# Zero products during the first loads, keys first, later rows' normalization behind the scores, and one bare step more at three places of the chains

## The chip, the cores and the metric

The kernel runs on one core of one Trainium2 chip. The core has a matrix engine (TensorE, called PE in the profile), a vector engine (VectorE, DVE), an activation engine (ScalarE, ACT), a general engine (GpSimd, POOL) and an engine that mainly starts transfers (SyncE, SP). Each works off its own queue in order and waits for the others by semaphores. Products land in PSUM, a small memory of banks from which DVE or ACT has to fetch them before a bank can be used again. The metric is the device time of one execution in microseconds (us).

## The reference

Two layers of a perceiver. x has 16 batches of 64 rows of 256 numbers, the context 16 batches of 1024 rows of 256. There are 16 heads of 16 numbers each.

```
x = x + cross_attention_0(layernorm(x), ctx, mask)      # softmax(q k / sqrt(16)) v, then Wout
x = x + column_attention(layernorm(x))                  # softmax with 1 + sum, rotary, causal
x = x + moe(layernorm(x))                               # 8 experts, 2 of them for each row, by capacity
x = x + cross_attention_1(layernorm(x), ctx, bias, mask)
x = x + row_attention(layernorm(x))                     # within each batch of 64 rows, rotary
x = x + fp4_feed_forward(layernorm(x))                  # silu(gate) * up, operands rounded to fp4 by blocks of 16
```

All is float32; the fp4 step is a rounding of float32 numbers to a grid of eight magnitudes, with a scale for each block of 16.

## The kernel before, in words

The 1024 rows of x are eight tiles of 128 rows, a tile being two batches (a pair). The layers follow each other: layer 0's cross attention (about 38 to 520 us of the profiled execution), column attention (to about 650), the experts (to about 870), then layer 1's cross attention, into which the row attention and the feed forward of finished pairs are woven (to about 1425), and a tail of what the last pairs still need.

**The order of work.** PE's order in the cross attention is the order in which the code issues it (the engine is under `manual_schedule`). The other engines' queues are ordered by a scheduler. Where the code says `issue_after`, an instruction's place is put behind a named other one.

**The main loop** of `cross_attention` (L331 to L761, the loop at L719) runs over 64 slots, four to a batch b: two halves of the heads (dt) by two halves of the keys (hf). One turn of the loop issues
- `scores` of the slot two ahead: four products (L567) into four banks, and for each a DVE instruction (L578) that adds the mask and finds the extremum (tile mn). Each second slot has also the four exponentials on ACT (L589);
- four k-steps of its own slot: `transpose_keys` (four transposes L597 into one bank, fetched by DVE at L226 or by ACT at L228), each followed by `advance()`. Between them come steps of projections for later batches: `project` (L394 for keys, L409 for values), or in layer 0 for most batches `project_seven` (L458, L462), a product by seven products instead of eight that needs sums of context made by POOL (`sum_context`, L448);
- `attend` of the slot before (L611, 32 products into the accumulating bank).

Seven banks go round among all users, and one is kept for `attend`.

**The chains.** `advance()` takes one step of every running chain. A chain is a Python generator, and each of its `yield`s leaves PE to one k-step of the loop before the chain's next piece; `bare(n)` (L250) is n yields with nothing between. The chains are
- `queries(n)`: `layernorm_rows` (L255: bn_stats at L258, bn_aggr at L260, three Newton steps for the inverse root, the rows xnq at L275 on DVE or L281 on POOL), two transposes (L290, fetched by ACT at L292), the query product (L527) and qm on ACT (L537), which the scores of the next pair need. It starts at the third of a pair's eight slots for the pair after;
- `outputs(b)` (L619) after a batch's last `attend`: ot, the transposes L633, osb (L636), and for the second batch of a pair some bare yields, the transposes L648, oT on DVE (L652), two yields, and `project_rows` (L322), the output product that goes into x;
- in layer 1 then `row_attention(n)` (qkv at L1371, L1391 and L1414, scores L1426, exponential ra on ACT at L1444, transposes L1450, L1465, L322 again) and `feed_forward(n)` (normalization, fp4 rounding on DVE, transposes L290, the hidden products L1517 in two halves, Silu on ACT (L1520), the product with up on DVE (L1521), fp4 rounding (L1036 to L1052), transposes L1527, the down product L1542).

exp and Silu are functions of different tables on ACT, and each change between them issues an ACT_TABLE_LOAD.

**Layer 0's end.** When the slots are finished, the remaining chain goes on with prepared layer-1 projections between its steps (`idle`, which calls `make_ahead`, L782 and L795); keys and values of most batches of layer 1 are prepared in this way or during the column attention. In layer 1 the remaining batches' projections (L394, L409) stand in the main loop: the later four pairs have them, the first three have not.

**The start.** The first loads are issued by ACT's and SP's queues: the key half of the weights w_L_xattn_Wkv, the first rows of x, column constants, the query weights, the value half, and the first context. Then, in PE's order: the first projection step (L394) of batch 0, a step of `queries(0)` (transposes L290), the second projection step, the rest of `queries(0)`, the scores of slots 0 and 1, and the other six steps (two for keys, four for values).

Of the kernel before, what the change touches and what calls it, by code (L numbers as in the profile page):

```python
# [9 lines left out]
F32 = mybir.dt.float32  # L10
# [110 lines left out]
def kernel(ctx: ExitStack, tc: tile.TileContext, a: dict, out: bass.AP):  # L121
# [17 lines left out]
    def bank():  # L139
        return psum["w"].tile([P, 512], F32, name="psw")  # L140
# [46 lines left out]


    w0kv = wpool.tile([P, KC, 2 * D], F32, name="w_L0_xattn_Wkv")
    w0kv_in = a["L0_xattn_Wkv"].rearrange("(c p) n -> p c n", p=P)  # L190
    nc.scalar.dma_start(w0kv[:, :, :D], w0kv_in[:, :, :D])
    nc.scalar.dma_start(x[0], xf[:P, :])
# [57 lines left out]
    def bare(n):  # L250

        for _ in range(n):
            yield

    def layernorm_rows(pool, n, name="xnr", vector=False):  # L255

        st = small.tile([P, 6], F32, name="bnst")
        nc.vector.bn_stats(st, x[n])  # L258
        mv = small.tile([P, 2], F32, name="mvr")
        nc.vector.bn_aggr(mv, st)  # L260
        va = small.tile([P, 1], F32, name="var")
        nc.vector.tensor_scalar(va, mv[:, 1:2], EPS, None, ALU.add)

        half = small.tile([P, 1], I32, name="half")
        nc.vector.tensor_scalar(half, va.bitcast(I32), 1, None, ALU.logical_shift_right)
        r = small.tile([P, 1], F32, name="rsd")
        nc.vector.tensor_scalar(r.bitcast(I32), half, -1.0, 1597463007.0, ALU.mult, ALU.add)
        t = small.tile([P, 1], F32, name="nwt")
        xn = pool.tile([P, D], F32, name=name)
        if vector:  # L270
            nc.vector.tensor_scalar(va, va, -0.5, None, ALU.mult)
            for _ in range(3):
                nc.vector.tensor_scalar(t, r, va, r, ALU.mult, ALU.mult)
                nc.vector.scalar_tensor_tensor(r, t, 1.5, r, ALU.add, ALU.mult)
            made[name] = nc.vector.tensor_scalar(xn, x[n], mv[:, 0:1], r, ALU.subtract, ALU.mult)  # L275
            return xn
        for _ in range(3):
            nc.gpsimd.tensor_scalar(t, r, va, r, ALU.mult, ALU.mult)
            nc.gpsimd.tensor_scalar(t, t, -0.5, 1.5, ALU.mult, ALU.add)
            nc.gpsimd.tensor_tensor(r, r, t, ALU.mult)  # L280
        made[name] = nc.gpsimd.tensor_scalar(xn, x[n], mv[:, 0:1], r, ALU.subtract, ALU.mult)  # L281
        yield
        yield
        yield
        return xn
# [45 lines left out]
    def cross_attention(layer, wq, wkv, wo, bq, bk, bv, bo, mask, keep, bias, after, ready, arrive, idle):  # L331
        side = "right" if layer else "left"
        with ExitStack() as st:
# [180 lines left out]
            def queries(n):  # L514


                arrive(n, two, 1)
                xn = yield from layernorm_rows(single, n, "xnq", layer == 1 or n == 0)
                if layer:
                    nc.gpsimd.tensor_tensor(x[n], x[n], rowbias(bo), ALU.add)  # L520
                    yield from bare(6 if n else 0)
                xT = transposed_rows(single, xn, "xTq")
                yield from bare(3 if layer else 2)
                pm = bank()
                for dt in range(KC):
                    for c in range(KC):
                        nc.tensor.matmul(  # L527
                            pm[:, dt * P : (dt + 1) * P],
                            wq[:, c, dt * P : (dt + 1) * P],
                            xT[:, c, :],  # L530
                            start=(c == 0),
                            stop=(c == KC - 1),
                        )
                qm[n] = two.tile([P, KC, 2, 2, SQ], F32, name="qm")
                for dt in range(KC):
                    for j in range(2):
                        nc.scalar.activation(  # L537
                            qm[n][:, dt, :, j, :],
                            pm[:, dt * P : (dt + 1) * P].rearrange("p (b q) -> p b q", q=SQ),
                            AF.Identity,  # L540
                            scale=const("parq")[:, j : j + 1],
                            bias=bqm[:, j, dt : dt + 1],
                        )
# [10 lines left out]
            def scores(b, dt, hf):  # L554
# [19 lines left out]
                for g in range(NG):  # L574
                    pr = dt * NG + g
                    e = es[b, dt, g]

                    nc.vector.tensor_tensor_reduce(  # L578
                        out=e[:, cols],
                        in0=sc[g],  # L580
                        in1=negb[b][:, cols],
# [37 lines left out]
            def outputs(b):  # L619
# [21 lines left out]
                    )  # L641
                if half == 0:
                    return
                yield from bare(3 if layer else 2)
                pt = bank()
                rows = osb[n].rearrange("p r j d -> p (r j d)")
                for c in range(KC):
# [2 lines left out]
                for c in range(KC):  # L650
# [1 line left out]
                    nc.vector.tensor_scalar(  # L652
                        oT[:, c, :], pt[:, c * P : (c + 1) * P], colbias(bv, c), None, ALU.add
                    )
                yield
                yield
                project_rows(n, oT, wo, None if layer else rowbias(bo))


# [39 lines left out]
            with tc.manual_schedule(engines={mybir.EngineType.PE}):  # L699
                arrive(0, two, 0)  # L700
                chains.append(queries(0))
                if 0 not in ready:
                    project(0, 0)
                    advance()
                    project(0, 1)
                while chains:
                    advance()
                if not layer:
# [5 lines left out]
                scores(*slots[0])  # L714
                scores(*slots[1])
                if 0 not in ready:
                    for step in range(2, NP):
                        project(0, step)
                for i in range(len(slots) + 1):  # L719

# [628 lines left out]
    def last_layers(one):  # L1349
# [148 lines left out]
        def feed_forward(n, two):  # L1498
# [4 lines left out]
            yield from fp4(fp4_tiles(one, "h", NI), xn, xn, P, D)  # L1503
            yield from bare(2)
            xT = transposed_rows(two, xn)
            yield
            yield
            h = one.tile([P, NI], F32, name="h")
            hT = one.tile([P, NCH, P], F32, name="hT")

# [174 lines left out]
```

## Time and profile before

| what | value |
|---|---|
| median of 3 runs | 1512.32 us (1509.17 to 1513.48) |
| profiled execution, its own time | 1521.49 us |
| its span, first to last instruction | 1519.5 us |
| PE busy in the span | 92% |
| DVE busy | 63% |
| ACT busy | 49% |
| POOL busy | 22% |
| mean granted PE clock | 0.955 |
| first matmul | 7.18 us |
| main loop of layer 0 begins | 38.10 us |
| table loads on ACT | 22 |

How to read it: times in the profile are microseconds from the first instruction of the profiled execution, which took 9.17 us more than the median of the runs. Differences inside the profile are taken from it alone, and only the sum is set against the median. A line of a timeline gives the start, the duration of a group of equal instructions, the engine, the line of the code, the operation, what it writes and reads, shapes, and the count; in brackets stand the idle time ahead of it and what ended that. The granted clock is 1.00 at full rate. A matmul of float32 is recorded as several passes, so that one projection step shows as four matmuls.

### The profile page before, as it was taken

What the parts mean: (1) busy time and instruction counts of PE and PEld (TensorE: products, weight loads), DVE (VectorE), ACT (ScalarE), POOL (GpSimd) and SP (SyncE); (2) the same over time, 40 slices, a digit from 0 to 9 for tenths busy, and PEclk for the clock granted to TensorE, in tenths of its full rate; (3) what the DMA queues carried; (4) which work ended last, traced back from release to release, by engine and by line L of the source; (5) the groups of instructions that cost most, each with busy time, mean ns of one, the idle gap of its engine ahead of it and who ended that gap; (6) DMA issues with size and microseconds to landing.
All of it is one profiled execution on the core that took longest, in us unless ns stands there. A gap on an engine that the chain in (4) does not pass through costs nothing.

```text
span 1519.5 us, 33552 instructions
## 1 busy us (share of the span) xinstructions
PE 1391.2 (92%) x13796; PEld 994.4 (65%) x13796; DVE 961.1 (63%) x2573; ACT 744.7 (49%) x1373; POOL 338.5 (22%) x368
## 2 busy tenths in 40 slices
PE   6999999999999898899999888979799999999854
PEld 3677667776777655668888555756566767676642
DVE  3677676767677524355730167587878687877654
ACT  2565566566665632123221376546565556565420
POOL 4343444344332021012300121111221111110000
PEclk9999999999999999999999899788999999999967
DMA  6111111121001122276882533222211111100000
GB/s 232 60 35 34 60 33 33 36 60 32 33 30 36 56 92 71 93 236 212 260 303 92 180 108 99 75 80 89 78 46 49 50 53 49 43 5 1 5 1 7
DMA packets 53557, 119.53 MB, mean 79 GB/s; under 512 B 4909, under 2 KB 25005, under 8 KB 51101
## 3 DMA queue, kind: packets, MB, share of 16 engines
q1 hardware_dynamic: 50732, 112.21, 22.4%
q0 software_dynamic: 1568, 4.26, 1.0%
q8 instruction: 108, 1.77, 0.5%
q10 hardware_dynamic: 1104, 0.93, 0.2%
q14 instruction: 45, 0.36, 0.1%
HBM read 94.32 MB, written 23.07 MB: 77 GB/s over the span
## 4 chain that ended last, share of the span: by engine, by line
PE 70%; DVE 16%; issue 5%; ACT 5%; DMA 3%; POOL 1%; ACTq 0%; DVEq 0%; POOLq 0%; SPq 0%
PE psw L597 10%; PE psw L567 8%; PE pso L611 7%; PE psw L458 6%; DVE e L578 5%; PE psw L462 5%; PE psw L795 4%; PE psw L1226 4%; PE psw L1246 4%; ACT e L589 4%; PE psw L394 3%; PE psw L782 3%; PE psw L1517 3%; PE psw L409 2%; PE psw L1542 2%
## 5 line engine op out<-in xcount | busy, mean ns | idle before, releaser
L589 ACT ACTIVATE e<-e,mn 128x1024 f32<-128x1024 f32 x256 | 291.1, 1139 | 119.1 <-DVE mn L578 119.1
L597 PEld LDWEIGHTS psw<-consts,e 128*128 128x128 f32 x2048 | 240.3, 143 | 102.9 <-issue 58.5
L597 PE MATMUL psw<-consts,e 128*128 128x128 f32 x2048 | 288.2, 279 | 10.5 <-ACT e L589 5.8
L228 ACT COPY eT<-psw 128x512 f32<-128x512 f32 x384 | 209.5, 588 | 176.3 <-PE psw L597 176.0
L578 DVE CUSTOM_DVE_ANT_0 e<-psw,negb,mn 128x512 f32<-128x512 f32 x256 | 178.5, 747 | 144.7 <-PE psw L567 144.7
L578 DVE CUSTOM_DVE_ANT_0 e<-psw,negb 128x512 f32<-128x512 f32 x256 | 163.8, 685 | 67.9 <-PE psw L567 67.4
L567 PE MATMUL psw<-kT,qm 32*128 32x512 f32 x1024 | 171.9, 659 | 11.1 <-ACT qm L537 6.6
L611 PE MATMUL pso<-eT,v 128*32 128x128 f32 x4096 | 140.9, 280 | 0.0
L611 PEld LDWEIGHTS pso<-eT,v 128*32 128x32 f32 x4096 | 106.2, 111 | 22.3 <-issue 21.9
L567 PEld LDWEIGHTS psw<-kT,qm 32*128 32x128 f32 x1024 | 53.5, 190 | 48.8 <-issue 20.1
L226 DVE COPY eT<-psw 128x512 f32<-128x512 f32 x128 | 82.8, 680 | 3.4 <-PE psw L597 3.4
L795 PE MATMUL psw<-w_L_xattn_Wkv_w,actx 128*128 128x256 f32 x288 | 74.6, 413 | 1.5 <-ACT astage L789 0.8
L359 POOL TENSOR_SCALAR negb<-m 128x1024 f32<-128x1024 uint8 x16 | 16.7, 1045 | 253.1 <-DVE mn L578 202.8
L782 PE MATMUL psw<-actx,w_L_xattn_Wkv_w 128*128 128x512 f32 x144 | 67.4, 608 | 1.3 <-DVE x L768 1.3
L795 PEld LDWEIGHTS psw<-w_L_xattn_Wkv_w,actx 128*128 128x128 f32 x288 | 58.7, 208 | 14.8 <-issue 4.2
L789 ACT ACTIVATE astage<-psw,colb 128x512 f32<-128x512 f32 x36 | 24.6, 686 | 80.8 <-PE psw L782 46.8
L462 PEld LDWEIGHTS psw<-wgT,actx 128*128 128x128 f32 x448 | 53.3, 192 | 10.6 <-issue 5.3
L462 PE MATMUL psw<-wgT,actx 128*128 128x128 f32 x448 | 58.3, 278 | 0.0
L1226 PE MATMUL psw<-xeT,w 128*128 128x256 f32 x256 | 56.6, 379 | 0.8 <-issue 0.8
L1246 PE MATMUL psw<-w,hT 128*128 128x256 f32 x256 | 56.6, 379 | 0.0
L458 PE MATMUL psw<-actx,wgT 128*128 128x512 f32 x112 | 56.4, 605 | 0.0
L1233 ACT ACTIVATE hT<-psw 128x512 f32<-128x512 f32 x32 | 19.0, 597 | 75.4 <-PE psw L1226 75.4
(282 smaller groups left out, 2281.2 us busy)
## 6 DMA issues: line engine op xcount, KB each, us to landing
ctxT<-in_ctxT_dram SPq DMA_DIRECT2D x23, 1024.0 KB, 4.8
w<-in_L_ffn_w_dram SPq DMA_DIRECT2D x16, 1024.0 KB, 8.3
actx<-in_ctxT_dram SPq DMA_DIRECT2D x9, 1024.0 KB, 5.6
kd<-astage SPq DMA_DIRECT2D x36, 256.0 KB, 4.4
vd<-astage SPq DMA_DIRECT2D x36, 256.0 KB, 2.3
kT<-kd SPq DMA_DIRECT2D x9, 1024.0 KB, 7.0
v<-vd SPq DMA_DIRECT2D x9, 1024.0 KB, 4.7
ab<-in_fside_BxS_dram SPq DMA_DIRECT2D x32, 256.0 KB, 3.3
```

What stands on the lines that cost most here:

```text
L228: nc.scalar.copy(dst, src)
L458: nc.tensor.matmul(pm, a_, x_, start=True, stop=True)
L462: nc.tensor.matmul(pm[:, cols], x_[:, cols], a_, start=True, stop=True)
L567: nc.tensor.matmul(sc[g], qm[b // 2][r : r + 32, dt, b % 2, :, :].rearrange("p j q -> p (j q)"), kT[b][r : r + 32, dt, cols], start=True, ...
L578: nc.vector.tensor_tensor_reduce(out=e[:, cols], in0=sc[g], in1=negb[b][:, cols], scale=1.0, scalar=3e38 if hf == 0 else mn[b][:, 0, pr : ...
L589: nc.scalar.activation(e, e, AF.Exp, scale=-1.0, bias=mn[b][:, 1, pr : pr + 1], accum_out=sums[b][:, pr : pr + 1])
L597: nc.tensor.transpose(pt[:, g * P : (g + 1) * P], es[b, dt, g][:, k * P : (k + 1) * P], ident)
L611: nc.tensor.matmul(po[b][32 * g : 32 * g + 32, dt, :], v[b][:, k, pr * 32 : (pr + 1) * 32], e[:, g, :], start=(k == 0), stop=(k == NK - 1),)
L782: nc.tensor.matmul(pm, w1kv[:, c, dt * P : (dt + 1) * P], actx[b][:, c, cols], start=(c == 0), stop=(c == KC - 1),)
L795: nc.tensor.matmul(pm[:, j * D : (j + 1) * D], actx[b][:, c, (k + j) * P : (k + j + 1) * P], w1kv[:, c, D : 2 * D], start=(c == 0), stop=( ...
L1226: nc.tensor.matmul(ph[:, j * CAP : (j + 1) * CAP], w1[:, c, (f + j) * P : (f + j + 1) * P], xeT[:, c, :], start=(c == 0), stop=(c == KC - 1),)
L1246: nc.tensor.matmul(py[:, j * D : (j + 1) * D], hT[:, f, j * P : (j + 1) * P], w2[:, f, :], start=(f == 0), stop=(f == FF // P - 1),)
```

## The change

There are four edits.

1. At the start of layer 0 three products of a tile of zeros are issued on PE into fresh banks ahead of the first projection. The tile is set by a DVE memset, which is the first instruction of DVE's queue. Nothing reads these banks before they are used again.
2. The first two projection steps come ahead of the transposes of `queries(0)`, and the third comes right after them; five instead of six steps follow the first scores.
3. In layer 0 the bn_stats of rows 1 to 7 (`layernorm_rows`) are put behind the last L578 that had been issued when `queries(n)` was started (`made["sc"]`).
4. Three numbers of bare steps grow by one: in layer 0 ahead of the transposes L648, in layer 1 ahead of `project_rows` of the cross attention (L322), and in `feed_forward` ahead of the hidden products (L1517).

```diff
     w0kv = wpool.tile([P, KC, 2 * D], F32, name="w_L0_xattn_Wkv")
+    zeros = wpool.tile([P, 1, P], F32, name="zeros")
+    nc.vector.memset(zeros, 0.0)
...
-    def layernorm_rows(pool, n, name="xnr", vector=False):
+    def layernorm_rows(pool, n, name="xnr", vector=False, behind=None):
         st = small.tile([P, 6], F32, name="bnst")
-        nc.vector.bn_stats(st, x[n])
+        with tc.issue_after(behind.ins) if behind else nullcontext():
+            nc.vector.bn_stats(st, x[n])
...
                 arrive(n, two, 1)
-                xn = yield from layernorm_rows(single, n, "xnq", layer == 1 or n == 0)
+                xn = yield from layernorm_rows(
+                    single, n, "xnq", layer == 1 or n == 0, made["sc"] if n and not layer else None
+                )
...
-                    nc.vector.tensor_tensor_reduce(
+                    made["sc"] = nc.vector.tensor_tensor_reduce(
...
                 if half == 0:
                     return
-                yield from bare(3 if layer else 2)
+                yield from bare(3)
                 pt = bank()
...
-                yield
-                yield
+                yield from bare(3 if layer else 2)
                 project_rows(n, oT, wo, None if layer else rowbias(bo))
...
                 if 0 not in ready:
+                    for _ in range(3):
+                        nc.tensor.matmul(
+                            bank().rearrange("p (k n) -> p k n", n=P),
+                            zeros[:, 0, :],
+                            zeros.to_broadcast([P, 4, P]),
+                            start=True,
+                            stop=True,
+                        )
                     project(0, 0)
+                    project(0, 1)
                     advance()
-                    project(0, 1)
+                    project(0, 2)
...
                 if 0 not in ready:
-                    for step in range(2, NP):
+                    for step in range(3, NP):
                         project(0, step)
...
             xT = transposed_rows(two, xn)
-            yield
-            yield
+            yield from bare(3)
             h = one.tile([P, NI], F32, name="h")
```

## The prediction

> **What bounds the kernel now.** I read the page first, then busy time by stretches, then the waits of TensorE (PE) in the two attention stages, then the first 40 us and the last 65 us instruction by instruction, and last ScalarE's (ACT's) table loads.
>
> ```profile
> PE 1391.2 (92%) x13796; PEld 994.4 (65%) x13796; DVE 961.1 (63%) x2573; ACT 744.7 (49%) x1373; POOL 338.5 (22%) x368
> ```
>
> ```profile
> core 0: us, PE busy (x) PEld busy (x) DVE busy (x) ACT busy (x) POOL busy (x), PEclk, DMA share, GB/s
> 24.00:30.00 6.00, 6.00 (x8) 2.19 (x7) 3.65 (x12) 4.33 (x7) 2.65 (x12) 0.50 0.84 310
> 120.00:400.00 280.00, 274.69 (x2792) 200.30 (x2795) 201.70 (x492) 173.52 (x327) 115.38 (x111) 1.00 0.13 40
> 1430.00:1520.00 90.00, 51.05 (x444) 34.60 (x443) 44.13 (x135) 15.56 (x28) 2.90 (x4) 0.74 0.02 5
> ```
>
> PE is the bound: 92% busy overall, 98% in the first cross attention (120 to 400). There a microsecond of PE waiting is a microsecond. From 1430 it is half idle, and chains of dependent steps set the time.
>
> ```profile
> 7.18 3.78 PE L394 MATMUL psw<-ctxT,w_L_xattn_Wkv 128*128 128x512 f32 x4 [7.18 <-DMA w_L_xattn_Wkv<-in_L_xattn_Wkv_dram]
> ...
> 12.85 0.69 PE L290 MATMUL psw<-consts,xnq 128*128 128x128 f32 x2 [1.90 <-DVE xnq L275]
> 13.34 3.38 PE L394 MATMUL psw<-ctxT,w_L_xattn_Wkv 128*128 128x512 f32 x4
> 16.55 1.05 PE L527 MATMUL psw<-xTq,w_L_xattn_Wq 128*128 128x128 f32 x8
> 18.50 1.99 PE L567 MATMUL psw<-kT,qm 32*128 32x512 f32 x14 [0.90 <-ACT qm L537]
> 23.19 2.07 PE L567 MATMUL psw<-kT,qm 32*128 32x512 f32 x2 [2.69 <-DVE mn L578]
> 25.19 6.07 PE L394 MATMUL psw<-ctxT,w_L_xattn_Wkv 128*128 128x512 f32 x8
> 31.10 7.07 PE L409 MATMUL psw<-w_L_xattn_Wkv,ctxT 128*128 128x256 f32 x32
> 38.10 1.14 PE L567 MATMUL psw<-kT,qm 32*128 32x512 f32 x8
> ```
>
> The start: PE begins when the first weights land (7.18), multiplies slowly, waits 1.90 for normalized rows and 2.69 for the first maximum of VectorE (DVE), and reaches the main loop at 38.10. Four matmuls of a projection (one step) take 3.78 or 3.38 here, 1.98 once the granted clock is full; the row 24 to 30 shows 0.50 granted.
>
> ```profile
> PE psw L648 <- DVE osb L636: 9.3, 7, 1.3
> ...
> PE psw L322 <- DVE oT L652: 12.0, 7, 2.2
> PE psw L1517 <- ACT xTr L292: 11.1, 6, 4.1
> PE psw L567 <- ACT qm L537: 4.8, 4, 2.2
> ```
>
> PE's waits (total, times, longest), the first of layer 0 (40 to 540), the others of layer 1 (900 to 1425). The first three waiters are moved.
>
> ```profile
> L1520 ACT ACT_TABLE_LOAD x8 | 10.3, 1283 | 0.1
> L589 ACT ACT_TABLE_LOAD x6 | 7.7, 1283 | 0.1
> ```
>
> ```profile
> 1474.36 0.53 ACT L228 COPY hT<-psw 128x256 f32<-128x256 f32 x2 [5.45 <-PE psw L1527]
> 1474.91 1.28 ACT L1444 ACT_TABLE_LOAD   x1
> 1476.20 1.06 ACT L1444 ACTIVATE ra<-ra 128x1024 f32<-128x1024 f32 x1
> 1477.31 1.97 PE L1450 MATMUL psw<-consts,ra 128*128 128x128 f32 x8 [2.99 <-ACT ra L1444]
> ```
>
> A table load (1283 ns) accompanies each change between exp and Silu. In the tail the last pair's exp (1476.20) holds PE's L1450.
>
> **The change, part by part.**
>
> *Start.* Three products of zeros are 6 matmul records at about 0.85 (L394's slow rate), an estimate of 5.1 us, before 7.17 when PE only waits; they need one DVE memset, so they cost nothing unless the memset comes after 2. Two steps now stand ahead of the transposes L290, so the 1.90 wait is filled. The later rows' bn_stats come behind the first scores' L578, so DVE (BATCH_NORM rows until 22.44) is free for the first scores at once. If the clock is full when the weights land: steps 0 and 1 from 7.18 to 11.2 (2 x 1.98), L290 at 12.85 (xnq ends at 12.80), step 2 to 15.3, L527 to 16.4, qm (1.5 in ACT, 17.64 to 19.14 before) with its 0.9 wait, scores from 17.3, paced at the end by the bank that the first L578 frees (18.0 + 0.7), done at 19.3. One key step (1.98) and four value steps (7.07 / 4) remain, and the main loop begins at 28.2 instead of 38.10: 9.9 won. If the clock stays slow until 14, the two steps end at 14.7, L290 and step 2 follow, and the gain is 8; if slow until 25, only the two waits and some 0.5 of overlap go: 5. Bounds 5 and 10.5; I take 9.9, since the zeros fill the stretch in which PE was idle.
>
> The Trainium skill, "TensorE: Matmul & The Clock Gate", Part 1, says that idling is the throttled default and that one busy free-running window of about 3.4 us releases it. The trace agrees in part: the clock is half from 23.17 to 29.99 in pieces of 3.41 us, after the idle 2.69. By that rule 5.1 us of zeros need not hold a whole window, and the start would go between the first two cases above.
>
> *Layer 0, L648 (seven pairs).* The transposes move past 16 L611 products, 4 L567, 8 L462 and one group of 4 transposes L597, over 3 us, and osb was 1.3 late: 9.3 removed. L322 follows two steps later as before, but oT (L652) now queues among L578: PE wants it at about 120.3 of the pair around 120, oT comes at 120.5 to 120.8, so 0.3 each. The normalization of rows 1 to 7 now runs in the rows' own slot: xnq (1.22 on GpSimd, POOL) ends, by POOL's order with L490 (1.27) ahead of it, at about 127.9, while PE wants L290 at 127.9 to 128.4: 0.2 each, and qm behind it 0.1. Net 9.3 - 7 x 0.6 = 5.1. Bounds: +9.3 if neither waits; -6 if both wait 1.1 more (a POOL operation's 1.22). Before, the rows lay ready a slot group ahead. At the end of layer 0 L322 has one prepared step more ahead of it and one less behind: bounds 0 and -1.7 (one step), I take -0.3, as 2 follow still. SP's and POOL's queues keep their DMAs but for small swaps.
>
> *Layer 1, L322 and L1517.* By pair L322 waits 1.02, 2.23, 2.23 and then 1.61 four times; L1517 waits 4.09 twice and 0.73 four times. In the four later pairs a slot also carries projection steps of nearly 2 us (L394, L409), so one yield more covers either wait: 4 x (1.61 + 0.73) = 9.4. In the early pairs L322 passes only one group of 4 transposes (0.44): 3 x 0.44 = 1.3; L1517 passes two such groups, L611 (1.08) and L567 (1.07), some 2.9 of its 4.09: 5.8. But there DVE and ACT are nearly as full and the next wait is theirs (L567 for qm already: 4.8), so I count half, 3.5, between 0 and 7.1.
>
> *Table loads.* In the changed order the second half's Silu falls behind the exps of the next slot: the program has 34 loads for 22, 12 more of 1.283 = 15.4 us of ACT, all in layer 1. ACT has slack there (49% overall), and qm (L537) behind a load is wanted some 3 us later in the projecting pairs; two early pairs lose 1.5 each: -3. Bounds 0 and -15.4.
>
> *Tail.* PE's order puts row 7's L1371, L1450 and L1465 ahead of row 6's L1517, L1542: L1450 comes 0.6 earlier, L1465 3.2, against chain steps of row 6 that come later. Bounds -1 and +5; I take +1.5, as row 6's down products (3.74) must still be done.
>
> **The sum.** 9.9 + 5.1 - 0.3 + 9.4 + 3.5 - 3 + 1.5 = 26.1. The profiled execution took 1521.49 (span 1519.5 and 2 around it), so 1495.4; it lies 9.17 above the median of 1512.32, whence 1486.2.
>
> **Rivals.**
> (A) Layer 1's gain is handed back: L1517 and L322 stop waiting, but PE next waits for banks that ACT and DVE free. DVE's waits for L567 there (a row of 66.6 us) speak against it, DVE is fed by PE; the early pairs speak for it. Without 9.4 + 3.5, less the loads' -3 now counted inside: 1486.2 + 9.9 = 1496.
> (B) All table loads on the path: 15.4 - 3 = 12.4 more than summed, 1498.6. For: four exps in a row ahead of a load leave Silu's two banks held, and PE has seven. Against: the exps there already end well ahead of PE in the projecting pairs.
> (E) A switch costs ACT twice its load, and all of it is on the path: 12 x 2 x 1.283 = 30.8, less 3, and 1514: within the measurement's bound. Against: between copy and exp in the rows above (1474.89 to 1476.20) lies nothing but the load.
> The Trainium skill, "ScalarE: Activation LUTs", "What ACT_TABLE_LOAD costs", speaks for (E): it gives about 1283 ns for the load and 1380 ns of drain, 2.66 us a switch, so 32 us for 12 (an estimate). The rows agree on the 1283 and show no drain.
> (C) Slower. Rows' normalization behind the scores makes xnq late at L290 for rows 2 to 7. PE's order is fixed, so all waits behind it. POOL decides: if sum_context's L448 products (5.1 us, 126.40 to 131.53) go ahead of xnq, six rows lose 5.1 each, 30.6, and 1517; with two L490 (2.55) more, 1532. It turns slower from 4.4 us a row on (26.1 / 6). For: the slack now used up was a slot group. Against: by POOL's order L448 stands behind xnq.
> (D) The zeros do not release the clock, so the start wins 5: 1491.
>
> **How the numbers follow.** Chances: forecast 0.47, A 0.17, B 0.09, C 0.10, D 0.15, E 0.02. The forecast's own range, from the terms' bounds taken in part, is 1478 to 1493. Leaving out half of C and the extremes of the others gives 1477 to 1508. A measurement here tells 0.3% (4.5 us) from no change: faster is under 1507.8, slower over 1516.9. A, D and the forecast are faster (0.79), B by half (0.04); the rest of B, E and a little of C fall within, C's rest (0.09) over it: 0.83 faster, 0.08 within, 0.09 slower.
>
> **What would show it.** L394 at 7.18 taking about 2 us for 4, the first L578 near 18 and the main loop near 28; L648 gone from layer 0's waits, no row of L290 waiting for xnq over 0.5 there; L322 and L1517 shrunk to the early pairs; 34 table loads, and L567's wait for qm grown by 3 at most; the last L1465 some 3 us nearer to row 7's scores. Wrong it would be by a row of L290 on POOL's xnq of tens of microseconds, or by L567 or L597 waiting for exps in layer 1.

## The result and the profile after

| | before | changed |
|---|---|---|
| median of 4 runs | 1512.9 us (1509.17 to 1521.0) | 1495.5 us (1492.21 to 1497.05) |
| profiled execution's span | 1519.5 us | 1490.3 us |
| table loads on ACT | 22 | 34 |

The changed kernel takes 0.9875 of the time, with a 95% interval of 0.9831 to 0.9919: faster by 1.2%. The forecast was 1486.2, in a range of 1477 to 1508. So the sign and the range held, and the gain is two thirds of the 26.1 us that were forecast. The two profiles are 29.2 us apart, against 17.4 of the medians; the section on the prediction comes back to this.

Lines of the changed kernel are shifted: L567 is now L574, L578 is L585, L597 is L604, L648 is L655, L322 is L326, L394 is L398, L1517 is L1531, L1527 is L1541 and L1542 is L1556; L290 is L294, L611 is L618, L1450 is L1465 and L1465 is L1480. In the runs below a line can lie a few places off these.

The busy shares of the page, of the changed kernel:

```profile
PE 1387.3 (93%) x13802; PEld 993.2 (67%) x13802; DVE 940.0 (63%) x2574; ACT 763.3 (51%) x1385; POOL 339.7 (23%) x368
```

The timeline of PE at the start, of the changed kernel (start, duration, count, and in brackets the idle time ahead):

```profile
1.05 4.41 PE L710 MATMUL psw<-zeros 128*128 128x512 f32 x6 [1.05 <-DVE zeros L192]
7.13 3.70 PE L398 MATMUL psw<-ctxT,w_L_xattn_Wkv 128*128 128x512 f32 x8 [1.68 <-DMA w_L_xattn_Wkv<-in_L_xattn_Wkv_dram]
12.84 0.44 PE L294 MATMUL psw<-consts,xnq 128*128 128x128 f32 x2 [2.01 <-DVE xnq L279]
13.12 1.88 PE L398 MATMUL psw<-ctxT,w_L_xattn_Wkv 128*128 128x512 f32 x4
...
16.79 3.15 PE L574 MATMUL psw<-kT,qm 32*128 32x512 f32 x16 [0.90 <-ACT qm L544]
...
28.69 1.14 PE L574 MATMUL psw<-kT,qm 32*128 32x512 f32 x8
```

The main loop begins at 28.69 instead of 38.10. Eight matmuls of L398 take 3.70, where four took 3.78.

PE's waits of the changed kernel (total, times, longest), from 40 to 535 and then from 880 to 1400:

```profile
PE psw L604 <- DVE mn L585: 2.6, 1, 2.6
PE psw L604 <- ACT e L596: 2.1, 3, 0.8
```

```profile
PE psw L326 <- DVE oT L659: 6.5, 7, 1.7
PE psw L1556 <- ACT hT L231: 5.3, 5, 2.0
PE psw L294 <- DVE xnr L279: 4.1, 3, 2.5
PE psw L604 <- DVE mn L585: 2.8, 2, 1.4
PE psw L1429 <- ACT h L1534: 2.7, 2, 1.3
```

The seven waits of L648 (9.3) and the waits of L1517 (11.1) are gone, and L322's fell from 12.0 to 6.5; in the later pairs 0.6 of each is left. In place of them stand one wait of 2.6 of L604 in layer 0, and in layer 1 waits for hT (5.3) and for Silu (L1534, 2.7), both from ACT.

**Where the time went.** I took the same product in both traces (the first of each eighth of the `attend` products, the first of each stage) and compared when it starts:

| stretch | difference, us |
|---|---|
| to the first slot's `attend` | -9.4 |
| layer 0, first pair to sixth | -7.4 (-1.73, then -1.11 to -1.14 each) |
| layer 0, seventh and last pair, and its end | +4.2 (+2.9 in the seventh, in which a wait of 2.56 stands) |
| column attention to the start of layer 1's `attend` | -5.9 |
| layer 1, pair 0; 1; 2 and 3 | 0.0; -6.8; +4.65 |
| layer 1, pairs 4 to 6; 7 | -2.3; -2.9 |
| tail | -3.4 |

The -5.9 lie in stages that the change doesn't touch. Some 3.6 of them go with the granted clock: before the experts' products the same work took 37.0 us at 0.82 in the profile before, 33.4 us at 0.90 in the one after. Another 2.2 lie in the column attention, 45.0 and 42.8 us at 0.92 both times, and stay unexplained. Single profiles differ by about this much: l322_alone and ff_step_alone (below), which leave everything up to layer 1 as it was, take 3.0 and 3.6 us less than the kernel before from layer 0's last `attend` to layer 1's first.

### The profile page after: what moved, and what is told of

Its sections match the earlier page's. It is cut to its first block, busy times and chain, and to the rows that moved or that the text cites. A ratio compares the mean times of both kernels' runs of the same rounds, so it can differ in the third digit from the quotient of the medians.

```text
span 1490.3 us, 33558 instructions
## 1 busy us (share of the span) xinstructions
PE 1387.3 (93%) x13802; PEld 993.2 (67%) x13802; DVE 940.0 (63%) x2574; ACT 763.3 (51%) x1385; POOL 339.7 (23%) x368
## 4 chain that ended last, share of the span: by engine, by line
PE 42%; DVE 10%; ACT 6%; issue 4%; DMA 2%; POOL 1%; ACTq 0%; DVEq 0%; POOLq 0%; SPq 0%
ACT e L596 4%; PE psw L604 4%; PE psw L1241 4%; PE psw L1261 4%; PE psw L810 4%; PE psw L574 4%; PE pso L618 3%; DVE e L585 3%; PE psw L398 2%; PE psw L413 2%; PE psw L797 2%; PE psw L1531 2%; DMA kd<-astage 2%; PE psw L1556 1%; PE psw L326 1%
## 5 line engine op out<-in xcount | busy, mean ns | idle before, releaser
L604 PEld LDWEIGHTS psw<-consts,e 128*128 128x128 f32 x2048 | 238.5, 142 | 104.5 <-issue 52.9
L604 PE MATMUL psw<-consts,e 128*128 128x128 f32 x2048 | 286.9, 278 | 13.1 <-DVE mn L585 6.6
L585 DVE CUSTOM_DVE_ANT_0 e<-psw,negb,mn 128x512 f32<-128x512 f32 x256 | 178.3, 746 | 129.6 <-PE psw L574 129.3
L585 DVE CUSTOM_DVE_ANT_0 e<-psw,negb 128x512 f32<-128x512 f32 x256 | 163.2, 686 | 67.6 <-PE psw L574 67.1
L574 PE MATMUL psw<-kT,qm 32*128 32x512 f32 x1024 | 175.6, 666 | 5.5 <-ACT qm L544 4.4
L618 PE MATMUL pso<-eT,v 128*32 128x128 f32 x4096 | 142.6, 282 | 0.0
L618 PEld LDWEIGHTS pso<-eT,v 128*32 128x32 f32 x4096 | 107.3, 112 | 23.5 <-issue 20.9
L574 PEld LDWEIGHTS psw<-kT,qm 32*128 32x128 f32 x1024 | 56.2, 191 | 44.0 <-issue 19.0
L466 PEld LDWEIGHTS psw<-wgT,actx 128*128 128x128 f32 x448 | 53.3, 192 | 10.6 <-ACT eT L231 10.6
L1248 ACT ACTIVATE hT<-psw 128x512 f32<-128x512 f32 x32 | 19.0, 598 | 74.1 <-PE psw L1241 74.1
```

Source lines behind the costliest of these rows:

```text
L466: nc.tensor.matmul(pm[:, cols], x_[:, cols], a_, start=True, stop=True)
L574: nc.tensor.matmul(sc[g], qm[b // 2][r : r + 32, dt, b % 2, :, :].rearrange("p j q -> p (j q)"), kT[b][r : r + 32, dt, cols], start=True, ...
L585: made["sc"] = nc.vector.tensor_tensor_reduce(out=e[:, cols], in0=sc[g], in1=negb[b][:, cols], scale=1.0, scalar=3e38 if hf == 0 else mn[b ...
L604: nc.tensor.transpose(pt[:, g * P : (g + 1) * P], es[b, dt, g][:, k * P : (k + 1) * P], ident)
L618: nc.tensor.matmul(po[b][32 * g : 32 * g + 32, dt, :], v[b][:, k, pr * 32 : (pr + 1) * 32], e[:, g, :], start=(k == 0), stop=(k == NK - 1),)
```

## The experiments

Each kernel was run beside the kernel before on the same chip; the chips differ between the three groups of four, so the ratios are what is compared. "Gain" is (1 - ratio) x 1512.9.

| kernel | median us | ratio, 95% interval | gain us |
|---|---|---|---|
| changed kernel | 1495.5 | 0.9875 (0.9831 to 0.9919) | 18.9 |
| no_zeros | 1492.38 | 0.9856 (0.9824 to 0.9888) | 21.8 |
| no_behind | 1495.38 | 0.9859 (0.9826 to 0.9892) | 21.3 |
| no_ff_step | 1486.02 | 0.9804 (0.9773 to 0.9834) | 29.7 |
| start_only | 1503.37 | 0.9932 (0.9906 to 0.9958) | 10.3 |
| exp_for_silu | 1489.03 | 0.9853 (0.9825 to 0.9881) | 22.2 |
| no_ff_exp_for_silu | 1482.45 | 0.9806 (0.9777 to 0.9834) | 29.4 |
| ff_step_alone | 1508.0 | 0.9975 (0.9955 to 0.9995) | 3.8 |
| last_row_free | 1487.7 | 0.984 (0.9809 to 0.9871) | 24.2 |
| l322_alone | 1496.76 | 0.9872 (0.9848 to 0.9897) | 19.4 |
| no_keys_first | 1498.95 | 0.9878 (0.9854 to 0.9902) | 18.5 |
| ln_behind | 1478.28 | 0.9755 (0.9731 to 0.9779) | 37.1 |
| ff_late | 1479.53 | 0.9763 (0.974 to 0.9785) | 35.9 |

### The start: no_zeros, no_behind, no_keys_first, start_only

**no_zeros**

```diff
-    zeros = wpool.tile([P, 1, P], F32, name="zeros")
-    nc.vector.memset(zeros, 0.0)
...
-                    for _ in range(3):
-                        nc.tensor.matmul(bank()..., zeros[:, 0, :], zeros.to_broadcast([P, 4, P]), ...)
```

> The changed kernel without the three products of zeros. Theory (the zeros release the granted clock): the first four matmuls L398 at 7.1 take 3.4 to 3.8 us instead of some 1.9, and the main loop begins at 31 to 33 us instead of 28.69; the time is 2.5 to 4 us above the changed kernel's 1495.5. Rival (keys first and the free vector engine alone do it, the clock would have come by itself): main loop at 28.5 to 29.5, time unchanged within 1 us.

PE's timeline in no_zeros:

```profile
6.98 6.09 PE L396 MATMUL psw<-ctxT,w_L_xattn_Wkv 128*128 128x512 f32 x8 [6.98 <-DMA w_L_xattn_Wkv<-in_L_xattn_Wkv_dram]
12.91 0.38 PE L292 MATMUL psw<-consts,xnq 128*128 128x128 f32 x2
...
28.70 1.14 PE L572 MATMUL psw<-kT,qm 32*128 32x512 f32 x8
```

The zeros do release the clock: without them the two steps take 6.09 instead of 3.70. But the slow steps end just when the normalized rows come (12.8), so with the zeros PE only waits 2.01 there instead. The main loop begins at 28.70 and 28.69. The products of zeros are worth nothing in this order. My theory fell in the time and held in the clock.

**no_behind**

```diff
-                    single, n, "xnq", layer == 1 or n == 0, made["sc"] if n and not layer else None
+                    single, n, "xnq", layer == 1 or n == 0, None
```

> The changed kernel with the later rows' bn_stats where the scheduler puts them. Theory: the vector engine's normalizations stand ahead of the first scores again (first L585 at 22 instead of 17.4), so that the main loop begins at about 32.5 instead of 28.69 (+4); but the wait of 2.56 of L604 in the last pair of layer 0, where a bn_stats of the column attention waits 4.85 for GpSimd's x (L332) ahead of L585, goes (-2.6), since GpSimd no longer runs a row's normalization ahead of L332; the main loop's 62 us a pair stays within 0.2. Sum +1, about 1497. Rival (the wait for x comes from the step in outputs, not from the normalization): the 2.6 stays, sum +4, 1499.5.

DVE's and PE's rows in no_behind:

```profile
22.36 0.68 DVE L585 CUSTOM_DVE_ANT_0 e<-psw,negb 128x512 f32<-128x512 f32 x1
...
23.10 2.07 PE L574 MATMUL psw<-kT,qm 32*128 32x512 f32 x2 [4.43 <-DVE mn L585]
...
35.80 1.14 PE L574 MATMUL psw<-kT,qm 32*128 32x512 f32 x8
```

The main loop begins 7.1 later, more than the 4 expected: the idle 4.43 is followed by slow products again. The changed kernel's wait of 2.6 is gone, as the theory said. By the end of layer 0 2.7 of the 7.1 are left. The medians of the two kernels can't be told apart (intervals of about 5 us each side), so that edit 3 as a whole is not shown to win or lose.

**no_keys_first**

```diff
                     project(0, 0)
-                    project(0, 1)
                     advance()
-                    project(0, 2)
+                    project(0, 1)
...
-                    for step in range(3, NP):
+                    for step in range(2, NP):
```

> The changed kernel with the old order of the first steps (one key step, transposes L294, one key step, the rest), zeros and normalization behind the scores kept. Theory (keys first fills the wait for the normalized rows, 2 us; the normalization behind the scores gives the rest): main loop at 30.5 to 31 instead of 28.69, first slot's products L618 at 43.3 to 44 instead of 41.59; time +2, 1497. Rival (without keys first the zeros or the clock matter and the scores come late): main loop at 33 or later, +4 and more.

PE's timeline in no_keys_first:

```profile
6.95 1.98 PE L398 MATMUL psw<-ctxT,w_L_xattn_Wkv 128*128 128x512 f32 x4 [1.45 <-DMA w_L_xattn_Wkv<-in_L_xattn_Wkv_dram]
12.54 0.69 PE L294 MATMUL psw<-consts,xnq 128*128 128x128 f32 x2 [3.61 <-DVE xnq L279]
13.02 3.62 PE L398 MATMUL psw<-ctxT,w_L_xattn_Wkv 128*128 128x512 f32 x4
...
32.75 1.14 PE L574 MATMUL psw<-kT,qm 32*128 32x512 f32 x8
```

The loss at the start is 4.06, twice what the theory had and near the rival's. With one step PE idles for 3.61, and the next products run at half the clock: the granted clock reads 0.50 from 13.0 to 16.6. After the idle 2.01 of the changed kernel the clock stayed, and four matmuls take 1.88. In the time of the whole kernel the loss doesn't show (a gain of 18.5 against 18.9, with intervals of some 4 us to each side).

The length of an idle stretch does not decide this alone. In the same changed kernel the granted clock reads 0.50 from 1024.9 on, after an idle 2.02 ahead of L1556, and from 956.6 to 959.9 after an idle 0.96 ahead of L574, while after the wait of 2.56 at 421.40 it stays at 1.00. Why the 2.01 at the start did no harm is therefore not shown.

The Trainium skill, "TensorE: Matmul & The Clock Gate", Part 1, has the clock throttled after one idle window of about 3.4 us. The traces agree in part: the 3.61 is longer than such a window, but in no_keys_first the clock reads 0.50 from 11.14 on, 2.21 us after PE's last product, and the 2.02 and 0.96 are shorter still.

**start_only**

```diff
-                yield from bare(3)
+                yield from bare(3 if layer else 2)
                 pt = bank()
...
-                yield from bare(3 if layer else 2)
+                yield
+                yield
                 project_rows(n, oT, wo, None if layer else rowbias(bo))
...
-            yield from bare(3)
+            yield
+            yield
             h = one.tile([P, NI], F32, name="h")
```

> The changed kernel with all three numbers of bare steps as they were before: zeros, keys first and the normalization behind the scores alone. Theory: the start's 9.4 stays won, the seven waits of L655 in layer 0 (9.3) and the waits in layer 1 are as before, and the last pair's 2.6 may stay: 1503.5 to 1506. Rival (the start does it nearly all, and the bare steps give next to nothing): 1495 to 1499.

The gain is 10.3 (6.4 to 14.2), a little more than the 6.9 to 9.4 of the theory. In its profile the first `attend` comes 9.8 earlier than before, and in layer 1 each pair takes the time of before to 0.2 us. In layer 0 the pairs take 0.0 to 0.06 more than before, the seventh 0.4, against -1.1 in the changed kernel; the step ahead of L655 sets the two apart there. PE's waits in start_only, from 30 to 505:

```profile
PE psw L655 <- DVE osb L643: 9.3, 7, 1.3
PE psw L604 <- ACT e L596: 2.1, 3, 0.8
PE psw L294 <- POOL xnq L285: 0.6, 1, 0.6
```

The changed kernel's wait of 2.6 for L585 is not among them, though the normalization stands behind the scores here too. As no_behind has no such wait either, it takes both: the normalization behind the scores, and the step ahead of L655.

### The steps of the chains: no_ff_step, ff_step_alone, l322_alone, ff_late

**no_ff_step**

```diff
-            yield from bare(3)
+            yield
+            yield
             h = one.tile([P, NI], F32, name="h")
```

> The changed kernel with two bare yields instead of three ahead of the hidden products. Theory (the step brings table loads that hand its gain back): 22 table loads instead of 34; in each later pair L1531's wait of 0.73 comes back, and the waits of L1556 for hT (0.4 to 0.6) and some 0.5 of PE time that is busy but stalled go; in early pairs 4.1 comes back, and 2.0 (hT), 1.3 (Silu) and 1.3 (L1441) go. Net 0 to -1 in layer 1: 1494 to 1496. Rival (the step is worth the wait that it removes): +0.73 x 4 + 2 x 3 = +9, 1504.

The theory had 1494 to 1496, the rival 1504; both were wrong. The time is 10.7 us under the changed kernel's by the ratios, with intervals that do not overlap by much. Against no_zeros, which ran on the same chip and differs from the changed kernel in the zeros alone, it is 7.9 under. So the third of the bare steps loses about as much as the whole start wins. Busy time by stretches, the third, fourth and sixth pair of layer 1, first of the changed kernel, then of no_ff_step (span, PE busy, then the other engines, the granted clock, DMA):

```profile
966.54:1040.48 73.94, 65.27 (x669) 44.35 (x668) 54.03 (x172) 44.24 (x81) 13.01 (x14) 0.86 0.24 81
1040.48:1118.91 78.43, 69.76 (x686) 45.78 (x685) 57.12 (x179) 48.42 (x89) 16.33 (x16) 0.91 0.15 52
1200.39:1281.65 81.26, 80.25 (x766) 56.02 (x765) 59.64 (x181) 48.91 (x88) 13.03 (x14) 1.00 0.15 47
```

```profile
970.39:1038.23 67.84, 60.03 (x669) 40.83 (x668) 56.41 (x172) 41.34 (x79) 12.98 (x14) 0.92 0.24 88
1038.23:1113.04 74.81, 67.00 (x686) 43.67 (x685) 59.52 (x179) 45.52 (x87) 16.29 (x16) 0.93 0.16 54
1193.61:1274.17 80.56, 79.60 (x765) 55.75 (x764) 60.13 (x180) 45.90 (x86) 12.90 (x14) 1.00 0.14 47
```

The third and fourth pair lose 9.7 together, each later pair 0.7. In the early two the same matmuls take PE 8.0 us more (65.27 + 69.76 against 60.03 + 67.00), and its idle time only 1.7 more: PE is not so much waiting as running at a lower clock. This is no chance of one profile: the four profiled kernels that have both steps for all rows and Silu (changed, no_zeros, no_behind, no_keys_first) take 152.2 to 152.6 us for these two pairs, the five with L322's step but without the other for these rows (no_ff_step, l322_alone, last_row_free, ln_behind, ff_late) 141.7 to 142.7. From the clock column, which reads 1.00 or 0.50 and something between only where a window holds both, time at half rate is (1 - clock) x 2 x span: 20.7 + 14.1 = 34.8 us against 10.9 + 10.5 = 21.4.

**ff_step_alone** and **l322_alone** take the kernel before, with one of the two steps each:

```diff
-            yield
-            yield
+            yield from bare(3)
             h = one.tile([P, NI], F32, name="h")
```

> The kernel before with the one step more ahead of the hidden products and nothing else. Its order has 22 table loads, as many as before: the 12 more come only where this step and the one ahead of L322 stand together. Theory (the loads and the place behind four exps, not the step by itself, cost): the wait of L1517 (11.1) shrinks to 4 or less, and the time is 1505 to 1511. Rival (one step more is too late in itself): 1518 to 1523, with new waits for Silu, hT or L578.

```diff
-                yield
-                yield
+                yield from bare(3 if layer else 2)
                 project_rows(n, oT, wo, None if layer else rowbias(bo))
```

> The kernel before with the one step more ahead of project_rows in layer 1 (L322) alone; 22 table loads, as before. Theory (this step gives most of layer 1's gain, in the early pairs through the granted clock): by the profile of the version without the step ahead of the hidden products, the second pair (63.28) falls to 56.4, the third and fourth together from 147.7 to 142.7, each later pair from 82.10 to 80.57, and the end by some 2: 15 to 19 us in the profile, a median of 1494 to 1500. Rival (the forecast's size: 4 x 1.61 + 1.3 = 7.7, the rest came with the other edits or by chance of the clock): 1503 to 1506.

Alone the step ahead of the hidden products wins a little (3.8, interval 0.8 to 6.8; less than its profile's 10 us in layer 1), and loads no more tables; the wait of L1517 shrank to 8.2, not to the theory's 4. The step ahead of L322 wins 19.4 (15.6 to 23.0), more than twice the forecast's 7.7. Before's second pair and sixth, and then the second, third and sixth of l322_alone:

```profile
928.49:991.77 63.28, 57.07 (x633) 40.03 (x632) 43.23 (x129) 37.76 (x71) 13.23 (x14) 0.87 0.28 98
...
1221.59:1303.68 82.09, 79.75 (x765) 56.04 (x764) 62.40 (x180) 45.96 (x87) 13.36 (x14) 1.00 0.15 46
```

```profile
924.86:981.29 56.43, 51.67 (x633) 37.33 (x632) 41.15 (x129) 37.65 (x71) 13.05 (x14) 0.94 0.31 111
981.29:1048.99 67.70, 59.89 (x669) 40.88 (x668) 56.38 (x172) 41.35 (x79) 12.96 (x14) 0.92 0.25 89
1204.41:1284.96 80.55, 79.60 (x766) 55.77 (x765) 60.10 (x181) 45.91 (x86) 12.93 (x14) 1.00 0.15 47
```

In the second pair idle time falls by only 1.45 (6.21 to 4.76), but PE's busy time by 5.4, with the clock at 0.94 instead of 0.87. This too is more than chance: the nine profiled kernels with L322's step and Silu take 56.3 to 56.8 us for this pair at 0.94, the kernel before and start_only 63.3 and 63.1 at 0.87 and 0.86. Which idle stretch took the clock down is not shown. In the later pairs L322's step takes most of both waits, L322's and L1517's (2.34 idle to 0.95), so that there is little left for the other step. In the changed kernel the two steps together give less than L322's alone (10.75 us in layer 1's profile against 20.5): the gain of the step ahead of the hidden products turns into a loss when the other is there. Then Silu of the second half falls behind the exponentials of the next slot, with more table loads; which of the two costs is asked below.

**ff_late**

```diff
-            yield from bare(3)
+            yield from bare(3 if n > 2 else 2)
             h = one.tile([P, NI], F32, name="h")
```

> The changed kernel with the step ahead of the hidden products only for rows 3 to 7, not for 0 to 2. Theory (of the step's cost of 9.5, some 9.7 lie in the third and fourth pair, where Silu's place behind four exps makes idle stretches that the clock answers; the later pairs' loss of 0.69 each is made good by 2 at the end): third and fourth pair together 142 to 144 instead of 152.4, later pairs 81.26 as in the changed kernel, 1485.5 to 1487.5. Rival (the table loads cost all over): 1491 to 1494.

The third and fourth pair take 142.6 together as the theory said, and the later ones 81.27. The time is still lower than forecast, 0.9763: the tail is 2.5 shorter than the changed kernel's too (72.9 against 75.5). Against no_ff_step layer 1 takes 3.7 less in the profiles (606.4 and 610.1). So the step's loss lies in the early pairs, and for the rows from 3 on it does no harm as a whole.

### Loads or place: exp_for_silu, no_ff_exp_for_silu

ACT's rows in the changed kernel, from 1236.5 in the sixth pair:

```profile
1236.59 1.14 ACT L596 ACTIVATE e<-e,mn 128x1024 f32<-128x1024 f32 x1
1237.63 0.19 ACT L596 ACTIVATION_READ_ACCUMULATOR e<-e,mn 128x1 f32 x1
1237.84 1.28 ACT L1534 ACT_TABLE_LOAD   x1
1239.13 0.44 ACT L1534 ACTIVATE h<-psw 128x320 f32<-128x320 f32 x1
1239.47 1.50 ACT L544 ACTIVATE qm<-psw,bqm,consts 128x128 f32<-128x128 f32 x4
```

Silu's second half comes after four exponentials and a load, and qm behind it. To part the loads from the place, exp stands for Silu in both versions:

```diff
-                nc.scalar.activation(h[:, cols], pg, AF.Silu)
+                nc.scalar.activation(h[:, cols], pg, AF.Exp)
```

> The changed kernel with exp in place of Silu in the feed forward (the hidden numbers are then other ones; the operation has the same size), so that the activation engine never changes tables there: 7 table loads in the program instead of 34, the place of every product as in the changed kernel. Theory (the 12 more loads are what the step ahead of the hidden products costs): the loss of some 9.5 us against the version without that step vanishes, 1486 to 1488, and the waits of L1556 for hT and of L1429 for Silu shrink under 1 each. Rival (the cost is the place: Silu stands behind four exponentials of the next slot and holds two banks, loads or not): 1492 to 1496, and the waits stay.

> The control to it: the version without the step ahead of the hidden products, with exp in place of Silu as well (other hidden numbers, same size of the operation): 7 table loads instead of 22. Theory (the loads cost where the step made them fall on the path): the 15 loads of this version are hidden, 1484 to 1486, as far from the other as the loads leave: within 2 us of exp_for_silu. Rival (the place costs): 7 to 10 us faster than exp_for_silu. If loads cost wherever they are: 1475 to 1480.

Without the feed forward's loads the two still differ by 0.0047 of the time, 7.1 us, near the rival's 7 to 10; with them by 7.9 (no_zeros against no_ff_step) or 10.7 (the changed kernel against it). By these medians most of the loss is the place, and the loads' share, 0.8 to 3.6, is within the noise, for the intervals leave some 4 us to each side. The profiles share it out otherwise: layer 1 takes 612.9 us in exp_for_silu and 611.0 in its control, 1.8 apart, against 619.6 and 610.1 with Silu, 9.5 apart. The profiled run of exp_for_silu was the fastest of its six (1485.45, median 1489.03). So how much is the place and how much the loads stays open; the profiles show where either tells. The same three pairs of exp_for_silu, then of its control no_ff_exp_for_silu, and exp_for_silu's waits in layer 1:

```profile
963.53:1037.83 74.30, 65.59 (x669) 44.65 (x668) 54.09 (x172) 38.99 (x77) 13.07 (x14) 0.86 0.24 81
1037.83:1119.52 81.69, 72.82 (x685) 47.30 (x684) 57.21 (x179) 43.16 (x85) 16.40 (x16) 0.87 0.16 50
1199.89:1280.27 80.38, 79.72 (x766) 56.06 (x765) 59.28 (x181) 43.65 (x84) 12.83 (x14) 1.00 0.15 48
```

```profile
968.79:1036.25 67.46, 58.90 (x669) 40.09 (x668) 55.04 (x172) 38.90 (x77) 12.78 (x14) 0.95 0.25 89
1036.25:1111.48 75.23, 67.24 (x685) 43.78 (x684) 58.34 (x179) 43.07 (x85) 16.12 (x16) 0.93 0.18 54
1192.40:1273.34 80.94, 79.98 (x766) 56.05 (x765) 60.03 (x181) 43.26 (x84) 12.94 (x14) 1.00 0.14 47
```

```profile
PE psw L1441 <- DVE mn L585: 4.4, 4, 2.0
PE psw L1556 <- ACT hT L231: 4.0, 2, 2.0
```

In the third and fourth pair the loss (156.0 for the two, against 142.7 of the control) and the waits for hT (2 x 2.0) stay with no load at all: that is place, and clock. In the later pairs the step wins without loads (80.38 against the control's 80.94) and loses with two loads more per pair (81.26 against no_ff_step's 80.56). What exp_for_silu makes up for lies in its second pair (53.3 against 57.3) and in the tail (70.1 against 74.1).

### The wait in layer 0's seventh pair: last_row_free, ln_behind

The wait lies in the seventh of layer 0's eight pairs, in which the last row is normalized; the expectations call this pair the last. DVE's and POOL's rows of the changed kernel around the wait of 2.6:

```profile
418.11 1.22 POOL L285 TENSOR_SCALAR xnq<-x,mvr,rsd 128x256 f32<-128x256 f32 x1
...
419.30 0.73 POOL L332 TENSOR_TENSOR x<-x,prow 128x256 f32<-128x256 f32 x1
...
420.06 0.43 DVE L238 BATCH_NORM_STATS2 bnst<-x 128x6 f32<-128x256 f32 x1 [4.85 <-POOL x L332]
...
420.62 0.72 DVE L585 CUSTOM_DVE_ANT_0 e<-psw,negb,mn 128x512 f32<-128x512 f32 x1
...
421.40 0.66 PE L604 MATMUL psw<-consts,e 128*128 128x128 f32 x4 [2.56 <-DVE mn L585]
```

The scheduler has put a bn_stats of the column attention's normalization (L238) ahead of the scores' L585. It needs x from POOL (L332), and POOL does the last row's normalization first, which edit 3 moved here; without the step ahead of L655 the wait is not there (start_only). DVE idles for 4.85, and PE for 2.56. Two ways to take away what it waits for, both on no_ff_step:

```diff
-                    single, n, "xnq", layer == 1 or n == 0, made["sc"] if n and not layer else None
+                    single, n, "xnq", layer == 1 or n == 0, made["sc"] if 0 < n < NT - 1 and not layer else None
```

> The version without the step ahead of the hidden products, with rows 1 to 6 behind the scores but the last row (7) free, so that GpSimd has normalized it before the last pair. Theory (GpSimd's normalization ahead of x of L332 makes the vector engine's bn_stats wait 4.85 us ahead of L585): L604's wait of 2.56 in the last pair of layer 0 goes, the start is kept (main loop at 28.2 to 28.7, one small group of vector work more), 2.5 us under that version's 1486.0: 1483.5. Rival (another order of the vector engine waits as long elsewhere in the last pair): 1485.5 to 1487.

```diff
             st = small.tile([P, 6], F32, name="bnst")
-            nc.vector.bn_stats(st, x[n])
+            with tc.issue_after(made["sc"].ins):
+                nc.vector.bn_stats(st, x[n])
```

> The version without the step ahead of the hidden products, with the column attention's bn_stats (L238) put behind the last L585 of layer 0 as well, so that none of them can wait for GpSimd's x in front of a score. Theory (freeing the last row only moved that wait of 3.8 one pair ahead, because the scheduler still hoisted these bn_stats): no wait of L604 for L585 over 1 in layer 0, layer 0's loop ends 2.5 to 3 earlier (last pair 63 instead of 64.5 from its first product), the start of the column attention no more than 0.5 later: 1483 to 1484. Rival (the bn_stats are wanted at once at the end, the transposes L307 wait for them): the gain given back there, 1486.

In last_row_free the wait did not go; it is one pair earlier and 3.8 long, for the scheduler hoists other bn_stats of L238 there (DVE idles 5.91 for POOL's x ahead of one). The gain of 24.2 is no better than no_ff_step's 29.7, close to the rival. In ln_behind the wait is gone. PE's only waits over 0.2 there from 30 to 505:

```profile
PE psw L605 <- ACT e L597: 2.1, 3, 0.8
PE psw L641 <- ACT ot L231: 0.5, 1, 0.5
```

The column attention's transposes do not wait for it more than 0.4 each. The time is 1478.28, a ratio of 0.9755, the lowest of all kernels here: 7.4 below no_ff_step, more than the 2.5 expected. In the profiles the seventh pair takes 60.4 instead of no_ff_step's 64.5 us: the wait of 2.53 is gone, and with it 3.41 us at half the clock behind it. Another 1.6 lie in the last pair, where no_ff_step has 3.4 us at half clock (0.95 against 1.00 over the last 33 us). The rest differs in untouched stages, and another chip was used, so only about 4 of the 7.4 can be ascribed to the wait. ff_late and ln_behind together were not run.

## Why the prediction was right, and where not

- **The start.** Forecast -9.9, measured -9.4; the size held, the reason did not. Step "if the clock is full when the weights land" came true by the zeros, but it is not needed: the forecast let L290 come at 12.85 in any case and did not see that two slow steps end there as well. The gain is keys first (4.1 of it lost without) and the normalization behind the scores (7.1 lost without). The two losses add up to more than the 9.4 won, as both hold slow products after an idle stretch. Rival D had the zeros' failing as worth 5; they could fail at no cost.
- **L648 in layer 0.** 9.3 removed as forecast. New waits were put at 0.6 a pair; the pairs show -1.1 instead of -0.7, so 0.2. But the sum of layer 0 is -3.2 and not -4.8: the seventh pair takes 2.9 more instead of 1.1 less, with the wait of 2.6. In ln_behind, without that wait, layer 0's pairs take 7.9 less than before. The step was not run by itself; by the medians it adds nothing (start_only 10.3 and l322_alone 19.4 make up no_ff_step's 29.7, to some 6 us). Rival C named the right order on POOL (a row's normalization against other work) but the wrong victim: xnq was on time at L290 everywhere, and x was late for a bn_stats that the forecast did not follow, though the profile before had its small form at 122.42 (0.84 idle for POOL's x).
- **Layer 1, L322 and L1517.** The sum was -9.4 - 3.5 + 3 - 1.5 for loads and tail included, -11.4; the profile shows -10.75 and the forecast looks right there. That is luck, for its terms are not right. The four later pairs were to give 9.4 and gave 5.2; the early ones, loads included, were to give 0.5 and gave 2.2; the tail 1.5 and gave 3.4. L322's step, sized at 7.7 in full and 7.1 in the sum, is worth 19.4 alone; the step ahead of the hidden products, sized at 5.8 less 3 for the loads, costs 7.9 to 10.7 beside it. The step that failed is "In the early pairs L322 passes only one group of 4 transposes (0.44)": it priced idle time alone, while PE's clock in the three early pairs stood at 0.86 to 0.95, and 1.45 us less of idle time went with 5.4 us of faster products in one pair.
- **Table loads.** 34 as counted from the order. Priced at -3; by the medians they cost 0.8 to 3.6, by the profiles of layer 1 up to 7.7 (9.5 less 1.8). What brings them also brings Silu's place behind four exponentials, which costs in the early pairs with no load at all (13.3 us in the two); the forecast had it only as a reason for rival B ("leave Silu's two banks held").
- **Rival E**, twice the load for a switch: the Trainium skill, "ScalarE: Activation LUTs", "What ACT_TABLE_LOAD costs", gives 1380 ns of drain at a switch. In the rows of the sixth pair above the exponential's last part ends at 1237.82, the load starts at 1237.84 and Silu 0.01 after the load's end; the rows here show no drain.
- **Tail.** Forecast -1.5, measured -3.4; row 7's L1465 (now L1480) and L322 (now L326) come 5.0 and 3.2 earlier, counted from the tail's start.
- **From the profile to the median.** The forecast took 9.17 off as a constant. Before's profile lay 9.17 over its median and the changed one's 3.3 under its own (1492.21 against 1495.5): 29.3 between the profiled executions, 17.4 between medians. By the profiles' own terms the forecast of 26.1 was near, with 5.9 of the 29.3 in stages that were not touched. What it took for the kernel's time held an unlucky course of the clock, and the changed kernel's profile a lucky one. The two offsets together are more than the 8.7 by which the medians fall short of the forecast.

## What to carry to other kernels

Where PE's granted clock is below one in a stretch, an idle gap there is not priced by its length: count the time at half clock beside the waits, for a step that takes 1.45 us of idle time out of a pair may shorten it by 7. Two moves that each win can lose together when the second pushes an activation past the next batch of another table; read the order of the activation engine for the two at once, and price the place as well as the loads. When work is put later on one engine, follow everything else on that engine to its readers, those that a scheduler hoisted from the next stage too.

## What was not expected of the hardware

- PE's busy time for the same 633 matmuls was 57.07 us at a mean granted clock of 0.87 and 51.67 at 0.94, with a fall in idle time of 1.45 only. At half clock it spent 17.07 us of the one pair (948.18 to 955.01 and 965.25 to 975.49 in the profile before) and 6.83 of the other.
- Matmuls on zeros alone release the clock: after 4.41 us of them, products ran at full rate 1.68 us later (eight in 3.70), and without them at first slowly (eight in 6.09). What takes it back is not the length of an idle stretch alone: in the changed kernel it stayed after 2.01 and 2.56 and fell after 2.02 and 0.96.
- A single profiled execution could be 9 us off its kernel's median. The time goes with the mean granted clock: of 16 executions of the kernel before, those above 1518 us have 0.954 or 0.955, those under 1510 us 0.959 to 0.962.
